# M3 before M4 in the lower half of layers two and three of a graph network, with two small products issued at later steps

## The chip, the cores and the metric

The kernel runs on one core of a Trainium2 chip. The metric is device time in microseconds (us) of one launch, which computes all 16 batches; the profile is one execution taken by the hardware profiler. Engines are called as in the profile: PE (TensorE; PEld its weight loads), DVE (VectorE), ACT (ScalarE), POOL (GpSimd) and SP (whose queue issues most DMAs). All data are 32-bit floats.

## The reference

Inputs are nodes x (16 x 1024 x 128), a sparse-patterned adjacency adj (16 x 1024 x 1024) and the weights of two networks, each followed by a residual sum and a layer norm:

```python
# first network
degree = adj.sum(-1)[:, :, None]
h = einsum('bid,bij->bjd', x, adj) / degree
x = layernorm(x + relu(concat([x, h]) @ W.T + b))
# second network, four layers of this form
src_agg = einsum('bjv,bij->biv', nodes @ ws + bs, l2norm(adj, 2))   # rows normalised
dst_agg = einsum('bjv,bji->biv', nodes @ wd + bd, l2norm(adj, 1))   # columns normalised
nodes = tanh(concat([src_agg, nodes @ wn + bn, dst_agg]) @ wu + bu)
# layers three and four also get earlier features concatenated
x = layernorm(x + nodes)
```

Each batch thus needs two scaled copies of its adjacency: one with columns divided by their norms (`a` in the kernel), one transposed with rows divided by theirs (`at`). The norms come from sums of squares of the rows (`cols`, on ACT) and of the columns (`acc`, on POOL).

## The kernel before, in words

Batches run one after the other, and while one batch is in its layers two and three, the next one's adjacency is loaded, squared, summed and scaled. Order is written by hand for PE, DVE, ACT and POOL: every engine executes its instructions in the order in which the Python code issues them. The stages of a batch on PE are: messages and products of layer one, of layer two, of layer three, then the first network of the next batch (`pa`, L417 to L431), then messages and products of layer four.

**Messages** (`messages`, L488). For four groups of two node blocks a matmul `pt` (L498) makes the messages, DVE adds a bias (L501), giving the tiles `t`. Then DVE makes sums of message blocks that the products need: S3 (L515), S1 (L516, in place in `t`), S2 (L517), S4 (L518), in this order. Each holds two parts, SRC and DST, of 64 columns for each of four blocks: one for the row-normalised and one for the column-normalised adjacency. The functions called through `between` are issued after the DVE addition of a group: in layer three `sums3`, which waits for POOL's last sum of squares, transposes it (L261) and reduces it to `part` (L266).

**Products** (`aggregate`, L553). The adjacency product is done in a form of Strassen's and Winograd's, with seven products of half-size blocks (M1 to M4, Z11, Z12, Z21) over combined quarters (T on the column side, Q on the row side). PE's array is used in two halves of 64 columns: a list `upper` and a list `lower` of matmuls are zipped, and each step issues one matmul of each (L669 to L677). In the trace every such matmul is two records, so a step has two pairs of records. With n the number of feature tensors (1 in layer two, 2 in layer three, 3 in layer four), a stage begins with 2n `own` steps (the node's own term), followed by 24 steps. The upper half runs M1 in 8 steps, M2 in 8, the SRC part of M3 in 4, Z21; the lower half runs M4 in 8 steps (into the PSUM tile Ck), the DST part of M3 in 4 (into Dk), then Z12 and Z11. Event functions read results at steps counted from the end of the own steps: at 8 `m1_read` (L584, L585) and `m4_read` (L588, L589) on ACT, at 12 a copy of Dk into half of `e1` on ACT (L655), at 16 `m2_read` (L592 on DVE, L593 on ACT) and the sum of the two halves on DVE (L649), at 20 `m3_read` (L596, L597) and `second_half` (L600 takes Z1 out of its PSUM bank, L601, then tanh on ACT, L690). The last half ends with L679.

**Hooks** of a stage are functions that are issued at a step counted with the own steps. Layer two of each batch but the last has the sums for the next adjacency (`sums`, L233): for each of eight row blocks the squares on ACT (L248, and a copy with a sum, L245, for the first four), degrees on DVE (L247) for the other four, and running sums on POOL (L250, L252). Layer three has:

- step 1, `inverses3` (L284): the product `pc` of the column sums on PE, three small DVE operations (L290, L292, L297), and a power on POOL (L298), which gives the inverse norms of rows and columns;
- step 5, `factors`: DMAs of node blocks; three small DVE operations (L316, L317, L319), a DMA of the inverses to DRAM (L321) and two DMAs that spread them as the row `cinv` (L327);
- step 10, `factors_of_rows` (L300): `spread` on DVE (L303), its product `rp` on PE (through L179), and the copy `rinv` on DVE (L309);
- step 11 a transpose on DVE (L338), and at 12, 15, 19 and 25 four scalings each of the next adjacency by `cinv` on DVE (L333).

`rinv` is used first in layer four, where ACT scales rows with it (L454). The first product of `pa` writes the PSUM bank of Z1 and so waits for L600.

Of the kernel before, what the change touches and what calls it, by code (L numbers as in the profile page):

```python
# [15 lines left out]
NL = 4  # L16
# [7 lines left out]
def adj_resnorm_kernel(ctx: ExitStack, tc: tile.TileContext, x, adj, w0, b0, layers, out):  # L24
# [33 lines left out]
    nc = tc.nc  # L58
# [10 lines left out]
    NJ = NB // 2  # L69
# [103 lines left out]
    def small(name, shape=(K,)):  # L173
        return ps_s.tile([P, *shape], F32, tag="small", name=name)
# [6 lines left out]
    def product(name, i=None):  # L181
        if i is None:
            return ps_t.tile([P, HW], F32, tag="pt", name=name)
        return ps_p.tile([P, HW], F32, tag=f"p{i}", name=name)
# [115 lines left out]
    def row_inverses(b, inv):  # L300

        spread = one.tile([P, NH, G, BPH], F32, tag="own", name=f"sp{b}")
        nc.vector.tensor_mul(spread, inv[:, :NB].rearrange("p (h k) -> p h k", h=NH)[:, :, None, :]  # L303
                             .to_broadcast([P, NH, G, BPH]),
                             group[:, None, :, None].to_broadcast([P, NH, G, BPH]))
        pr = small(f"rp{b}")
        by_halves(pr, fold, spread.rearrange("p h g k -> p (h g k)"))
        rinv = one.tile([P, K], F32, tag="rinv", name=f"rinv{b}")
        nc.vector.tensor_copy(rinv, pr)  # L309
        return rinv  # L310
# [169 lines left out]
    def combine(i, y, T):  # L480
# [4 lines left out]
        else:  # L485
            nc.vector.tensor_sub(T[4], y[1, 0], T[2])

    def messages(b, l, feats, wm, between={}, with_sums=True):  # L488


        nch = CHUNKS[l]
        t = [one.tile([P, NJ, 2, 2, V], F32, tag=f"t{j}", name=f"t{l + 1}_{b}_{j}") for j in range(2)]
        for n, g in enumerate((2, 3, 0, 1)):
            pt = ps_t.tile([P, 2, 2 * P], F32, tag="pt", name=f"pt{l + 1}_{b}_{g}")
            for q in range(2):
                i = 2 * g + q
                for k, (f, c) in enumerate(feats):
                    nc.tensor.matmul(pt[:, q], f[:, i * P:(i + 1) * P], wm[:, 1 + c],  # L498
                                     start=(k == 0), stop=(k == nch - 1))
            j, o = divmod(2 * g, NJ)  # L500
            nc.vector.tensor_add(t[j][:, o:o + 2].rearrange("p k a v c -> p k (a v c)"), pt,  # L501
                                 wm[:, 0][:, None, :].to_broadcast([P, 2, 2 * P]))
            if n in between:
                between[n]()
        if not with_sums:
            return t


        s = slice(1 if l == 0 else 0, 2)
        S = {i: one.tile([P, NJ, 2, V], F32, tag=f"S{i}", name=f"S{i}_{l + 1}_{b}") for i in (2, 3, 4)}  # L510
        X = {(v, j): t[j][:, :, :, v] for v in range(2) for j in range(2)}
        S[1] = X[1, 0]
        if l == 0:
            nc.vector.tensor_sub(S[2][:, 0:2, 0], X[0, 0][:, 0:2, 0], X[1, 0][:, 0:2, 0])
        nc.vector.tensor_sub(S[3][:, :, s], X[0, 0][:, :, s], X[1, 0][:, :, s])  # L515
        nc.vector.tensor_add(S[1][:, :, s], X[1, 0][:, :, s], X[1, 1][:, :, s])  # L516
        nc.vector.tensor_sub(S[2][:, :, s], S[1][:, :, s], X[0, 0][:, :, s])  # L517
        nc.vector.tensor_sub(S[4][:, :, s], X[0, 1][:, :, s], S[2][:, :, s])  # L518
        return X, S

    SRC, DST = 0, 1

    def plain_layer(b, l, feats, t, a, at, fT, etag, hooks):

# [28 lines left out]
    def aggregate(b, l, feats, msgs, a, at, T, Q, fT, etag, hooks={}, pieces=1):  # L553


        w = wown[l]
        n = len(feats)
        X, S = msgs
        Y = {DST: quarters(a), SRC: quarters_t(at)}
        TT = {DST: T, SRC: Q}  # L560
        low, high = slice(0, V), slice(V, P)
        Z0, Z1 = (product(f"z{h}_{l}_{b}", h) for h in range(NH))
        A, Bk, Ck = (product(f"m{i}_{l}_{b}") for i in range(3))
        e0 = one.tile([P, HW], F32, tag="e0", name=f"e0_{l}_{b}")
        e12 = one.tile([P, 2, HW], F32, tag=etag, name=f"e12_{l}_{b}")
        e1, e2 = e12[:, 0], e12[:, 1]
# [7 lines left out]
        def prod(name, part):  # L574
            y, t = Y[part], TT[part]
            x, y = {"M1": lambda: (X[0, 0], y[0, 0]), "M2": lambda: (S[2], t[2]), "M3": lambda: (S[3], t[3]),
                    "M4": lambda: (S[1], y[0, 1]), "Z11": lambda: (X[0, 1], y[1, 0]),
                    "Z12": lambda: (S[4], y[1, 1]), "Z21": lambda: (X[1, 1], t[4])}[name]()
            return [(x[:, k, part], y[:, k]) for k in range(NJ)]
# [7 lines left out]
        def m4_read():  # L587
            nc.scalar.copy(e2[high], Ck[low])  # L588
            nc.scalar.copy(e2[low], Ck[low])  # L589
# [15 lines left out]
        if l == 0:  # L605
            upper = [
                (Z1, True, own(1, 1)), (Z0, True, own(1, 0)),
                (Z1, False, [src(1, 1, j) for j in range(2, NB)]),
                (A, True, prod("M1", DST)), (Bk, True, prod("M2", DST)), (A, True, prod("M3", DST)),
                (Z0, False, prod("Z21", DST) + [src(1, 0, j) for j in range(NB)]),  # L610
            ]
            lower = [
                (Z1, True, own(0, 1)), (Z0, True, own(0, 0)),
                (Z1, False, [(S[2][:, j, SRC], at[1][:, j]) for j in range(2)] + [src(0, 1, j) for j in range(2, NB)]),
                (Ck, True, prod("M4", DST) + [src(1, 1, j) for j in range(2)]),
                (Z1, False, prod("Z12", DST)),
                (Z0, False, prod("Z11", DST) + [src(0, 0, j) for j in range(NB)]),
            ]
            def m4_and_m2_read():
                m4_read()  # L620
                m2_read()

            def m3_and_second_half():
                m3_read()
                second_half()

            events = {10: m1_read, 14: m4_and_m2_read, 18: m3_and_second_half}
        else:
            Dk = product(f"m3_{l}_{b}")
            upper = [  # L630
                (Z1, True, own(1, 1)), (Z0, True, own(1, 0)),
                (A, True, prod("M1", DST) + prod("M1", SRC)), (Bk, True, prod("M2", DST) + prod("M2", SRC)),
                (A, True, prod("M3", SRC)),
                (Z0, False, prod("Z21", SRC) + prod("Z21", DST)),
            ]
            lower = [
                (Z1, True, own(0, 1)), (Z0, True, own(0, 0)),
                (Ck, True, prod("M4", DST) + prod("M4", SRC)), (Dk, True, prod("M3", DST)),
                (Z1, False, prod("Z12", SRC) + prod("Z12", DST)),
                (Z0, False, prod("Z11", SRC) + prod("Z11", DST)),  # L640
            ]

            def first_reads():
                m1_read()
                m4_read()

            def m2_and_half_of_m3():
                m2_read()
                nc.vector.tensor_add(e0[high], e0[high], e1[high])  # L649

            def last_reads():
                m3_read()
                second_half()

            events = {8: first_reads, 12: lambda: nc.scalar.copy(e1[high], Dk[low]), 16: m2_and_half_of_m3,  # L655
                      20: last_reads}

        def steps(groups, rows):
            flat = []
# [85 lines left out]
    inv = two.tile([P, C], F32, tag="inv", name="inv0")  # L745
# [152 lines left out]
    for b in range(B):  # L898
        nxt = b + 1 < B
        n = b + 1  # L900
        y, yt = quarters(a), quarters_t(at)
        st = {}
# [5 lines left out]
        if b == 0:  # L908
            def first_half0():
                nonlocal rinv  # L910
                to_x1(0)
                rinv = row_inverses(0, inv)
                column_reduce(0, st0, acct)
                for q in (2, 3):
                    scale_rows(rows[q], q, rinv)
# [38 lines left out]
            def folded(l, part):  # L954
                return lambda *_: part(l, fetched[l])

            hooks = {1: lambda *_: inverses(0, st0, NB), 3: rows0, 4: folded(1, fold_begin), 6: folded(1, fold_end),
                     7: cinv0, 9: lambda *_: fold_and_scale(2, 0), 11: second0, 12: folded(2, fold_end),
                     14: lambda *_: fold_and_scale(3, 1), 18: first0, 20: folded(3, fold_end), 26: sums0}
# [5 lines left out]
        else:  # L965
# [3 lines left out]
            w = {"ys": summed(f"y{nm}")}  # L969
# [24 lines left out]
            def end1(w=w):  # L994
# [3 lines left out]
            hooks = {0: begin1, 7: scale1, 12: centre1, 17: squares1, 19: rstd1,  # L998
                     22: lambda: combine_1(yt), 25: end1, 28: lambda: combine(2, yt, Q)}
# [13 lines left out]
        hooks = {0: quarters2}  # L1013
# [9 lines left out]
        w = {}  # L1023
# [13 lines left out]
            w["cinv"] = factor_row(n, st, 1, "cinv")  # L1037

        def factors_of_rows(w=w):
            w["rinv"] = row_inverses(n, st["inv"])  # L1040

        def scale(i, h):
            scale_columns(a2, w["cinv"], range(i, i + NJ), half(h))

        hooks, between = {}, {}
        if nxt:
            between = {1: sums3}
            hooks = {1: inverses3, 5: factors, 10: factors_of_rows, 11: start3, 12: lambda: scale(0, 1), 15: lambda: scale(NJ, 1), 19: lambda: scale(0, 0),
                     25: lambda: scale(NJ, 0)}
        t = messages(b, 2, feats, wm, between)  # L1050
        wm = message_weights(b, 3)
        aggregate(b, 2, feats, t, a, at, T, Q, f23, "acc", hooks)
        if nxt:
            dinv = factor_row(n, st, 2, "dinv")
            yT = first_gnn(n, w["xn"], w["xT"], a2, dinv)
            rinv = w["rinv"]
# [96 lines left out]
    b = B - 1  # L1153
# [48 lines left out]
```

## Time and profile before

| quantity | value |
|---|---|
| three timed runs | 2528.31, 2528.6, 2529.8 us; median 2528.6 |
| profiled execution | 2525.06 us, span 2523.3 us, granted PE clock 0.999 |
| busy: PE, DVE, ACT, POOL | 2498.0, 1652.3, 836.5, 523.8 us |
| products of layer one, in batches 1 to 14 | 27.85 us |
| products of layer two, all batches | 26.54 to 26.55 us |
| products of layer three, batches 0 to 14 | 27.92 to 29.28 us, mean 28.65 |
| the same in batch 15, which has no hooks there | 27.62 us |
| products of layer four, batches 0 to 14 | 29.43 us |

The stages are measured from their first matmul to that of the following stage, in the timeline of PE. In a line of the timeline stand start, duration, engine, line of the kernel, operation, output and input, number of instructions, and in brackets how long the engine had been idle and what ended that. In a line of the waits stand the waiting engine, tile and line, then the releasing engine, tile and line, total us, number of times and the longest. The chain of work gives start, duration and what ran. Batches are counted from 0.

### The profile page before, as it was taken

The page shows a single profiled execution, that of the slowest core. Times are in us where ns is not written, and L with a number is a line of the kernel's source. Part 1 is how long each engine was busy: PE and PEld are TensorE (multiplying, and loading weights), DVE is VectorE, ACT ScalarE, POOL GpSimd, SP SyncE. Part 2 cuts the span into 40 slices and gives each one's busy share as a digit, 9 for nine tenths or more (in the row PEclk, how much of TensorE's full clock was granted, in tenths as well). Part 3 has the DMA queues.
Part 4 walks back from the last instruction along what each step waited for, and adds up shares of the span by engine and source line. Part 5 has one row for each costly group of instructions (what it writes and reads, how often), then busy time and mean ns, then how long its engine had stood idle before and what let it go on. Part 6 is the DMA issues. An engine that isn't in the chain of part 4 may idle for free.

```text
span 2523.3 us, 30190 instructions
## 1 busy us (share of the span) xinstructions
PE 2498.0 (99%) x11693; PEld 1158.6 (46%) x11693; DVE 1652.3 (65%) x1982; ACT 836.5 (33%) x1553; POOL 523.8 (21%) x217
## 2 busy tenths in 40 slices
PE   8999999999999999999999999999999999999998
PEld 4544445444454444544435454344544445444454
DVE  5858566585665757667576575765758567585643
ACT  5414333142331513324133251432414333142311
POOL 5401204012040221302113030130301204012000
PEclk9999999999999999999999999999999999999999
DMA  9417254271543615436163451725417255271410
GB/s 203 98 44 148 53 99 99 51 143 40 101 101 68 129 34 109 99 65 125 34 124 83 84 107 47 132 64 100 95 45 148 53 97 102 51 143 40 92 23 9
DMA packets 358736, 219.63 MB, mean 87 GB/s; under 512 B 148929, under 2 KB 329409, under 8 KB 358593
## 3 DMA queue, kind: packets, MB, share of 16 engines
q1 hardware_dynamic: 357184, 213.51, 41.8%
q0 software_dynamic: 1408, 4.20, 0.7%
q8 instruction: 92, 1.51, 0.3%
q14 instruction: 52, 0.42, 0.1%
HBM read 199.17 MB, written 18.46 MB: 86 GB/s over the span
## 4 chain that ended last, share of the span: by engine, by line
PE 67%; DVE 9%; SPq 5%; POOL 5%; DMA 4%; issue 4%; ACT 4%; DVEq 0%; POOLq 0%; ACTq 0%
PE m L677 26%; PE z L677 19%; PE pt L498 10%; PE pa L179 8%; SPq L231 5%; DMA a<-in_adj_dram 3%; POOL acc L252 2%; PE pw L179 2%; POOL inv L298 2%; ACT sq L248 1%; DVE e L601 1%; DMA out_dram<-y 1%; POOL acc L250 1%; ACT sq L245 1%; DVE cols L247 1%
## 5 line engine op out<-in xcount | busy, mean ns | idle before, releaser
L375 POOL TENSOR_TENSOR rs<-ve,mhalf 128x32 f32<-128x32 f32 x30 | 162.8, 5428 | 1388.5 <-DVE ve L373 1388.5
L677 PE MATMUL z<-at,t 128*64 128x512 f32 x1224 | 383.7, 592 | 0.0
L677 PE MATMUL m<-Q,S 128*64 128x512 f32 x768 | 337.4, 592 | 0.0
L501 DVE TENSOR_TENSOR t<-pt,wm 128x512 f32<-128x512 f32 x256 | 175.4, 690 | 177.7 <-PE pt L498 177.3
L677 PE MATMUL m<-T,S 128*64 128x512 f32 x1008 | 290.9, 593 | 0.0
L677 PE MATMUL m<-a,t 128*64 128x512 f32 x1008 | 266.6, 594 | 0.0
L252 POOL TENSOR_TENSOR acc<-acc,sq 128x1024 f32<-128x1024 f32 x90 | 221.3, 2459 | 130.6 <-ACT sq L248 127.0
L677 PE MATMUL z<-a,S 128*64 128x512 f32 x504 | 228.3, 593 | 0.0
L677 PE MATMUL z<-a,t 128*64 128x512 f32 x504 | 226.8, 592 | 0.0
L677 PE MATMUL z<-T,t 128*64 128x512 f32 x504 | 226.8, 592 | 0.0
L454 ACT ACTIVATE a<-a,rinv 128x256 f32<-128x256 f32 x480 | 198.2, 495 | 54.9 <-DMA a<-in_adj_dram 47.0
L677 PE MATMUL m<-at,t 128*64 128x512 f32 x828 | 214.5, 593 | 0.0
L333 DVE TENSOR_TENSOR a<-a,cinv 128x512 f32<-128x512 f32 x250 | 156.5, 696 | 88.1 <-DMA cinv<-dr 84.4
L498 PE MATMUL pt<-wm,f1T 128*128 128x256 f32 x768 | 213.6, 383 | 0.1
L179 PE MATMUL pa<-a,xn 128*64 128x512 f32 x960 | 208.6, 592 | 0.2 <-DVE e L600 0.2
L677 PE MATMUL z<-at,S 128*64 128x512 f32 x444 | 200.8, 592 | 0.0
L584 ACT COPY e<-m 64x512 f32<-64x512 f32 x63 | 36.6, 582 | 473.5 <-PE m L677 473.1
L677 PEld LDWEIGHTS z<-at,t 128*64 128x64 f32 x1224 | 120.8, 137 | 130.7 <-issue 111.3
L677 PEld LDWEIGHTS m<-Q,S 128*64 128x64 f32 x768 | 105.2, 137 | 164.3 <-issue 146.2
L677 PE MATMUL z<-Q,t 128*64 128x512 f32 x384 | 172.6, 592 | 0.0
L677 PEld LDWEIGHTS m<-T,S 128*64 128x64 f32 x1008 | 102.4, 137 | 144.4 <-issue 123.9
L498 PEld LDWEIGHTS pt<-wm,f1T 128*128 128x128 f32 x768 | 143.3, 190 | 44.3 <-issue 19.9
(197 smaller groups left out, 3698.3 us busy)
## 6 DMA issues: line engine op xcount, KB each, us to landing
a<-in_adj_dram SPq DMA_DIRECT2D x120, 512.0 KB, 12.7
a<-in_adj_dram SPq DMA_DIRECT2D x480, 128.0 KB, 4.1
xn<-in_x_dram SPq DMA_DIRECT2D x128, 64.0 KB, 2.0
wm<-wsave SPq DMA_DIRECT2D x16, 512.0 KB, 3.8
wm<-wsave SPq DMA_DIRECT2D x31, 256.0 KB, 3.3
xs<-in_x_dram SPq DMA_DIRECT2D x60, 128.0 KB, 3.5
cinv<-dr SPq DMA_DIRECT2D x30, 256.0 KB, 5.1
dinv<-dr SPq DMA_DIRECT2D x30, 256.0 KB, 5.1
```

The source lines that it names most:

```text
L179: nc.tensor.matmul(out[s], x[:, s], y, start=start, stop=stop)
L231: nc.sync.dma_start(ov[g, :, ks], ys[g * C:(g + 1) * C, ks])
L245: nc.scalar.activation(sq, a[:, i, :], AF.Copy, accum_out=degree)
L252: nc.gpsimd.tensor_add(acc, acc, sq)
L298: nc.gpsimd.tensor_tensor(inv[:, s], cols[:, s], mhalf[:, s], ALU.pow)
L333: engine.tensor_mul(a[:, i, s], a[:, i, s], cinv[:, s])
L375: nc.gpsimd.tensor_tensor(rstd, ve, mhalf[:, :n], ALU.pow)
L454: nc.scalar.activation(st[:, k], st[:, k], AF.Copy, scale=rinv[:, q * QB + k:q * QB + k + 1])
L498: nc.tensor.matmul(pt[:, q], f[:, i * P:(i + 1) * P], wm[:, 1 + c], start=(k == 0), stop=(k == nch - 1))
L501: nc.vector.tensor_add(t[j][:, o:o + 2].rearrange("p k a v c -> p k (a v c)"), pt, wm[:, 0][:, None, :].to_broadcast([P, 2, 2 * P]))
L584: nc.scalar.copy(e0[high], A[high])
L677: nc.tensor.matmul(o, x, y, start=start, stop=stop)
```

## The change

In layers two and three the lower half takes the DST part of M3 first (4 steps) and then M4 (8 steps); layer four keeps M4 first. The reads at the events are exchanged with them: at 8, after `m1_read`, the copy of Dk; at 12 `m4_read`. S3 is made in two DVE operations, the DST part before the SRC part, in layers two, three and four (in layer one there is only the DST part, as before). In layer three, `inverses3` is issued at step 4 instead of 1; `row_inverses` is cut in two, with `spread` at step 10 as before and the product `rp` with the copy `rinv` at step 18, between the second and the third group of scalings.

```diff
         nc.vector.tensor_mul(spread, ...)
+        return spread
+
+    def gather_inverses(b, spread):
         pr = small(f"rp{b}")
         by_halves(pr, fold, spread.rearrange("p h g k -> p (h g k)"))
         rinv = one.tile([P, K], F32, tag="rinv", name=f"rinv{b}")
...
-        nc.vector.tensor_sub(S[3][:, :, s], X[0, 0][:, :, s], X[1, 0][:, :, s])
+        for part in (DST, SRC) if l else (DST,):
+            nc.vector.tensor_sub(S[3][:, :, part], X[0, 0][:, :, part], X[1, 0][:, :, part])
...
+            first_of_lower = [(Ck, True, prod("M4", DST) + prod("M4", SRC)), (Dk, True, prod("M3", DST))]
+            reads_of_lower = [m4_read, m3_half]
+            if l < NL - 1:
+                first_of_lower.reverse()
+                reads_of_lower.reverse()
...
             lower = [
                 (Z1, True, own(0, 1)), (Z0, True, own(0, 0)),
-                (Ck, True, prod("M4", DST) + prod("M4", SRC)), (Dk, True, prod("M3", DST)),
+                *first_of_lower,
...
             def first_reads():
                 m1_read()
-                m4_read()
+                reads_of_lower[0]()
...
-            events = {8: first_reads, 12: lambda: nc.scalar.copy(e1[high], Dk[low]), 16: m2_and_half_of_m3,
-                      20: last_reads}
+            events = {8: first_reads, 12: reads_of_lower[1], 16: m2_and_half_of_m3, 20: last_reads}
...
         def factors_of_rows(w=w):
-            w["rinv"] = row_inverses(n, st["inv"])
+            w["spread"] = row_inverses(n, st["inv"])
+
+        def factors_gathered(w=w):
+            w["rinv"] = gather_inverses(n, w["spread"])
...
-            hooks = {1: inverses3, 5: factors, 10: factors_of_rows, 11: start3, 12: lambda: scale(0, 1), 15: lambda: scale(NJ, 1), 19: lambda: scale(0, 0),
-                     25: lambda: scale(NJ, 0)}
+            hooks = {4: inverses3, 5: factors, 10: factors_of_rows, 11: start3, 12: lambda: scale(0, 1),
+                     15: lambda: scale(NJ, 1), 18: factors_gathered, 19: lambda: scale(0, 0), 25: lambda: scale(NJ, 0)}
```

More of the change, by code (lines that the diff above doesn't have):

```diff
@@ L486, in combine @@
             nc.vector.tensor_sub(T[4], y[1, 0], T[2])
+    SRC, DST = 0, 1
     def messages(b, l, feats, wm, between={}, with_sums=True):
@@ L519, in messages @@
         return X, S
-    SRC, DST = 0, 1
     def plain_layer(b, l, feats, t, a, at, fT, etag, hooks):
@@ L629, in aggregate, with m3_half @@
             Dk = product(f"m3_{l}_{b}")
+            def m3_half():
+                nc.scalar.copy(e1[high], Dk[low])
+            first_of_lower = [(Ck, True, prod("M4", DST) + prod("M4", SRC)), (Dk, True, prod("M3", DST))]
[3 more added lines that the diff above has]
+                reads_of_lower.reverse()
             upper = [
@@ L911, in first_half0 @@
                 to_x1(0)
-                rinv = row_inverses(0, inv)
+                rinv = gather_inverses(0, row_inverses(0, inv))
                 column_reduce(0, st0, acct)
```

## The prediction, as it was put down before the result was known

> **What bounds the kernel now.** I read the page's engine shares first, then the waits, then the timeline of one batch (number 2, layers two and three, from 398.97 us), then the chain of work at the end of its layer three.
>
> ```profile
> PE 2498.0 (99%) x11693; PEld 1158.6 (46%) x11693; DVE 1652.3 (65%) x1982; ACT 836.5 (33%) x1553; POOL 523.8 (21%) x217
> ...
> PEld rp L179 <- DVE sp L303: 18.1, 15, 1.3
> PEld pc L179 <- DVE part L266: 13.7, 15, 1.4
> DVE a L333 <- DMA cinv<-dr: 84.4, 15, 6.7
> ```
>
> TensorE is busy 99% of the span, so only its gaps can be won. Two waits stand once in each batch that prepares a next one (15): rp, the product of the row inverses, and pc, that of the column sums.
>
> ```profile
> 433.96 0.31 PE L179 MATMUL pc<-part,fold 128*64 128x32 f32 x4 [0.26 <-DVE part L266]
> ...
> 442.44 0.31 PE L179 MATMUL rp<-sp,fold 128*64 128x32 f32 x4 [0.40 <-DVE sp L303]
> ```
>
> Matmuls overlap, so bracketed idle time understates what is lost. Records of one half of the array start 0.43 us apart; upper and lower half run side by side. The pair before pc started at 433.10, so the next was due at 433.53: 0.43 lost. Before rp, 441.43 + 0.43 = 441.86: 0.58 lost. A third loss has no wait row:
>
> ```profile
> 399.81 0.69 DVE L515 TENSOR_TENSOR S<-t 128x512 f32<-128x512 f32 x1
> 400.53 0.69 DVE L516 TENSOR_TENSOR t<-t,t 128x512 f32<-128x512 f32 x1
> ...
> 400.74 3.82 PE L677 MATMUL m<-a,t 128*64 128x512 f32 x15
> ...
> 404.39 0.59 PE L677 MATMUL m<-a,t 128*64 128x512 f32 x1
> ...
> 436.71 3.61 PE L677 MATMUL m<-a,t 128*64 128x512 f32 x16
> ```
>
> In layer three 16 records of M1 and M4 start within 3.61 - 0.59 = 3.02 us; in layer two they need 404.39 - 400.74 = 3.65. M1 starts on time, but M4's operand (L516) ends at 401.22, so the lower half trails by 0.63 us, to the end of the stage: the layer-two products take 26.54 us in every batch, 60 pairs of records x 0.429 = 25.74.
>
> The last view shows what waits behind those gaps:
>
> ```profile
> 450.84 7.31 DVE L333 TENSOR_TENSOR a<-a,cinv 128x512 f32<-128x512 f32 x12 [6.70 <-DMA cinv<-dr]
> ...
> 460.35 0.69 DVE e L596
> 461.04 0.03 issue
> 461.07 0.70 DVE e L600
> 461.77 0.04 issue
> 461.81 1.50 PE pa L179 x5
> ```
>
> The next stage, pa, starts 0.05 us after L600, which frees its PSUM bank. L600 stands behind a chain on other engines: squares on ACT, sums on POOL (to 431.4), transpose, column sums, power on POOL, two DMAs, twelve scalings, L592, L649, L596.
>
> **What the Trainium skill says.** *SBUF — State Buffer*, "Who interferes with whom": a VectorE instruction with two SBUF inputs and a GpSimd instruction that reads SBUF exclude each other, the later one blocking for the whole of the earlier. The trace agrees: L601 takes 2.42 instead of 0.69 us where it meets a running sum of POOL (L252, 2.36). *VectorE: DVE Perf Modes*, "The DRAIN you can't avoid": the next operation waits until the pipe is empty, unless it is not held. Here waited neighbours L515 and L516 start 0.725 us apart for 0.69 of work, unwaited scalings 0.60.
>
> **The change, part by part.** The batches' stages are measured between first matmuls in the timeline.
>
> 1. *M3 first in layer two* (16 batches). M3's first products need only the DST half of S3: it begins at 399.81, takes 0.42 (the 128x256 form) and is there at 400.23, 0.5 before 400.74. M4 comes four steps (3.4 us) later, long after its operand. Gain on PE: 0.63 each. In layer three M4 wasn't late (its operand ended at 436.55, before 436.71), so there the swap gives nothing.
>
> 2. *The split of S3* in layers two to four: two of 0.42 for one of 0.69. Half to half isn't waited, some 0.33 apart, half to L516 0.45 (both from layer one's rows): 0.78 for 0.725, +0.06 on DVE. In layer four it hides under six own steps (5.1 us). In layer three it lies in the chain to L600.
>
> 3. *pc to step 4.* Part is finished 1.3 us after the stage begins, step 4 comes at 3.4: the wait goes. Its readers on DVE follow the S sums anyway (437.92), so nothing behind them moves.
>
> 4. *rp to step 18.* The spread is ready 9.8 us after the stage begins; step 18 comes at 15.5: the wait goes. Its copy to rinv (L309) now stands on DVE between scalings 8 and 9, ahead of L592 and L600: 0.11 us (from its start to the next operation's, as before). SP and POOL keep their order. pc and rp together: the stage lasts 28.65 us in the mean of the 15, against 27.62 in the batch without hooks plus 0.28 for the eight short matmuls: 0.75 each.
>
> 5. *The reads on ACT in layer two.* One copy (L655) stands where two stood (L588, L589), so the square behind it ends 0.60 earlier, while L593, behind all of them, keeps its time:
>
> ```profile
> 416.93 1.06 ACT L248 ACTIVATE sq<-a 128x1024 f32<-128x1024 f32 x1
> ...
> 418.10 0.62 ACT L593 COPY e<-e 64x512 f32<-64x512 f32 x1
> ...
> 416.44 7.66 POOL L252 TENSOR_TENSOR acc<-acc,sq 128x1024 f32<-128x1024 f32 x3 [2.27 <-ACT sq L248]
> ...
> 418.75 0.69 DVE L649 TENSOR_TENSOR e<-e,e 64x512 f32<-64x512 f32 x1 [3.31 <-ACT e L593]
> ...
> 422.23 2.42 DVE L601 TENSOR_TENSOR e<-e 128x512 f32<-128x512 f32 x1
> ```
>
> POOL's first sum would run 415.86 to 418.22, the second from about 418.3 to 420.65. L649 is released at 418.75, now inside the second (before, it slipped between two); it would end some 0.55 after it, 421.2 instead of 419.44. Batch 0 shows this meeting already: L649 takes 2.68 there. Behind it L247, L596 and L600 move 1.76 back, but L601 then meets no sum: 421.2 + 2.69 + 0.10 + 0.69 = 424.7, against 424.65. So the sharing takes the delay in, and the chain leaves layer two +0.05. Bounds: -0.6 if the earlier square is passed on whole, +1.76 if L649's delay is.
>
> *Sum.* PE alone would win 16 x 0.63 + 15 x 0.75 = 21.3 us. But pa can't start before L600. L600 ends before pa by 0.05 (batches 2 and 6) to 1.26 us, 0.83 in the mean; less the 0.05, 0.78 of room. Its chain hangs on layer one, by the load of the next adjacency and its squares, not on PE in layers two and three, so PE's gain doesn't move it; it grows by 0.05 + 0.06 + 0.11, with rounding 0.25. The gain per batch is the room less this: 0.53, or 15 x 0.53 = 8.0, less 0.1 for batch 1, where PE's own path ends last; plus 0.63 in the last batch, which has no chain: **8.5 us**. Against the profiled span, 2523.3 - 8.5 = 2514.8; the timed runs are 5.3 longer (median 2528.6), so 2520.1.
>
> **Rivals.**
> - *The full gain.* The chain shortens because squares and sums start earlier: at -0.4 per batch instead of +0.25, 0.65 x 15 more, capped by PE's path in several: 16 us in all, 2512.6. For it: POOL waits 2.27 and 2.48 us for squares. Against: the last two squares stand behind L601's tanh, which doesn't come earlier.
> - *No change.* The chain eats the room, growing 0.8 instead of 0.25: 15 x (0.78 - 0.8) + 0.6, about 2528. For it: DMA landings scatter (L600's place varies by 2.4 us over the batches). Against: no added work of that size.
> - *Slower.* On DVE in layer two POOL's next sum goes ahead of the waiting L649 once more, 2.36 us per batch, all of it in the chain: 15 x (0.78 - 0.25 - 2.36) + 0.6 = -26.8, 2555. Decides from a growth of 0.82 us (1.16 for 0.2%). Against: in batch 0 L649 got in after one sum.
> - *M3 doesn't start on DST alone*: if it waits for both halves (the second ends at 399.81 + 0.33 + 0.42 = 400.56, and a weight load is 0.14), the lower half trails by less than 0.1. Since L600 bounds nearly all batches, that costs under 0.5 us: 2520.5.
>
> **How the numbers follow.** 0.2% is 5.1 us, about what measurement can tell from no change. The forecast, with M3's rival, gets 0.57, its own range 2515.5 to 2524.5 (growth from 0 to 0.5); the full gain 0.14; no change 0.20; slower 0.09. Faster: 0.55 of the first and the full gain, 0.69; same 0.22; slower 0.09. The range leaves out the slower rival and the ends of the others: 2511 to 2527.5.
>
> **What would show it.** Right: layer two's products 25.9 us in place of 26.54; no waits of pc and rp; pa 0.05 us after L600 in nearly all batches, with PE's gap now there, in layer three; L649 near 2.4 us and L601 at 0.69 in layer two; L309 between scalings. Wrong: layer two still 26.5; L600 more than 0.5 us later against the start of layer two, or earlier (the full gain); new gaps in layers four or one, where nothing waits now.

## The result, and the profile after

The changed kernel takes 2519.31 us (median of 6 runs, 2518.91 to 2522.89) against 2528.45 us (6 runs, 2525.58 to 2529.91) of the kernel before, run beside it: a ratio of 0.9967, 95% interval 0.9954 to 0.998. It is faster, by 9.1 us; 8.5 were forecast. The profiled span fell less, from 2523.3 to 2517.5 us, because the profiled execution of the kernel before (2525.06 us) was faster than all its timed runs. In the two later measurements the same change gained 7.2 and 6.0 us (ratio 0.9975 in both).

Lines have moved by some: L588, L589 (reads of M4) are now L592, L593, the copy of Dk L655 is L636, the half sum L649 is L663, L592 and L596 are L596 and L600, L600 is L604, L601 is L605, the tanh L690 is L703, the matmuls of the products L677 are L690, the scalings L333 are L336, the copy to rinv L309 is L312. In text about a changed kernel the new numbers are used. The description counts 24 steps behind the own ones; they are 28 (Z21 and Z11 have eight), which with the two own steps of layer two makes the 60 pairs of records that the prediction counts with.

The page's engine shares, kernel after:

```profile
PE 2487.2 (99%) x11693; PEld 1051.9 (42%) x11693; DVE 1661.8 (66%) x2030; ACT 836.3 (33%) x1553; POOL 519.8 (21%) x217
```

DVE has 48 instructions more, the second halves of S3 in 16 batches and three layers. PE's busy time fell by 10.8 us with the same number of matmuls; 16 x 0.64 = 10.2 us is what layer two's products lost. The share of 99% says as little as before. The waits, kernel after (waiting engine, tile, line, then the releaser; total us, times, longest):

```profile
DVE a L336 <- DMA cinv<-dr: 91.9, 15, 7.5
...
ACT f23T L703 <- DVE e L605: 27.9, 32, 0.9
ACT e L636 <- DMA out_dram<-y: 26.6, 13, 3.0
...
PEld pa L179 <- DVE e L604: 23.4, 15, 2.8
...
PE pa L179 <- DVE e L604: 10.2, 14, 2.0
...
PEld pt L503 <- ACT f23T L703: 5.6, 11, 1.3
```

The rows in which pc waits for part and rp for sp are gone. In their place stands pa, 15 times, waiting for L604, the operation that frees Z1's bank (L600 before). PE's timeline in layer two of batch 2, which starts at 398.04:

```profile
399.80 0.59 PE L690 MATMUL m<-a,t 128*64 128x512 f32 x1
399.81 0.59 PE L690 MATMUL m<-T,S 128*64 128x512 f32 x1
400.23 0.59 PE L690 MATMUL m<-a,t 128*64 128x512 f32 x1
400.24 0.59 PE L690 MATMUL m<-T,S 128*64 128x512 f32 x1
```

Upper and lower half (M1 reads `a` and `t`, M3 `T` and `S`) now start 0.01 us apart, and stay so. DVE makes the two halves of S3 from 398.87 to 399.63. The products of layer two take 25.90 us in all 16 batches, against 26.54. The chain of work that ends with the start of pa, batch 2, kernel after (start, duration, what ran):

```profile
458.65 0.70 DVE e L663
459.35 0.03 issue
459.38 0.02 DVEq L600
459.40 0.04 issue
459.45 0.69 DVE e L600
460.14 0.03 issue
460.17 0.70 DVE e L604
460.87 0.04 issue
460.91 1.50 PE pa L179 x5
```

L604 ends at 460.87 and pa starts at once. Before, that held in 2 of the 15 batches that prepare a next one (0.83 us in the mean); now it holds in all 15 (0.06). So TensorE has become fast enough, and the chain on the other engines sets the time. The stages, mean of batches 0 to 14, us:

| stage | before | after |
|---|---|---|
| products of layer two | 26.54 | 25.90 |
| messages of layer three | 7.10 | 7.38 |
| products of layer three, with the wait ahead of pa | 28.65 | 28.62 |
| pa | 17.27 | 17.32 |
| products of layer four | 29.43 | 29.43 |

Layer one and four don't change. Layer two gives 0.64, but 0.28 of it come back in the messages of layer three (to 8.23 instead of 7.10 in batch 12): PE comes earlier to its wait for the tanh L703 (the row of pt above, L503 is the matmul of the messages), which still comes when L605 releases it. Layer three takes as long as before: what pc and rp no longer cost is waited for ahead of pa. The four stages add up to 79.56 us before and 79.22 after; unrounded they differ by 0.355. With the last batch (0.64) that is 15 x 0.355 + 0.64 = 6.0 us. The profiled execution after reached its first layer two 0.2 us later (90.11 instead of 89.93), which leaves the 5.8 us by which the spans differ.

The link in layer two that the prediction worked out (item 5) reads like this, in views of batch 2. ACT before, with the two copies of M4 ahead of the next square:

```profile
412.90 0.58 ACT L588 COPY e<-m 64x512 f32<-64x512 f32 x1
413.49 0.58 ACT L589 COPY e<-m 64x512 f32<-64x512 f32 x1
413.97 1.05 ACT L245 ACTIVATE sq<-a 128x1024 f32<-128x1024 f32 x1
```

ACT after:

```profile
411.51 0.58 ACT L636 COPY e<-m 64x512 f32<-64x512 f32 x1 [1.69 <-DMA out_dram<-y]
412.10 1.06 ACT L245 ACTIVATE sq<-a 128x1024 f32<-128x1024 f32 x1
...
413.28 1.06 ACT L248 ACTIVATE sq<-a 128x1024 f32<-128x1024 f32 x1
...
416.69 0.62 ACT L597 COPY e<-e 64x512 f32<-64x512 f32 x1
```

POOL and DVE after:

```profile
414.57 7.57 POOL L252 TENSOR_TENSOR acc<-acc,sq 128x1024 f32<-128x1024 f32 x3 [3.47 <-ACT sq L248]
```

```profile
417.34 2.58 DVE L663 TENSOR_TENSOR e<-e,e 64x512 f32<-64x512 f32 x1 [2.84 <-ACT e L597]
...
421.93 0.69 DVE L604 TENSOR_TENSOR e<-e,z 128x512 f32<-128x512 f32 x1
422.72 0.69 DVE L605 TENSOR_TENSOR e<-e 128x512 f32<-128x512 f32 x1
```

L663 is released inside POOL's second sum and takes 2.58 us in place of 0.69; L605, which took 2.42 before, takes 0.69. The work on the next row block starts 0.59 us behind the first copy instead of 1.07, so 0.48 earlier (in all 15 batches), not 0.60. From the first copy of the lower half on ACT to the end of L605, batches 1 to 14 take 11.90 us in the mean, against 11.74.

### The profile page after: what moved, and what is told of

The parts are those of the page before. It is cut to its first block, busy times and chain, and to the rows that moved or that the text cites. A ratio compares the mean times of both kernels' runs of the same rounds, so it can differ in the third digit from the quotient of the medians.

```text
span 2517.5 us, 30270 instructions
## 1 busy us (share of the span) xinstructions
PE 2487.2 (99%) x11693; PEld 1051.9 (42%) x11693; DVE 1661.8 (66%) x2030; ACT 836.3 (33%) x1553; POOL 519.8 (21%) x217
## 4 chain that ended last, share of the span: by engine, by line
PE 59%; DVE 12%; DMA 9%; SPq 7%; ACT 4%; POOL 4%; issue 2%; DVEq 0%; POOLq 0%; ACTq 0%
PE m L690 22%; PE z L690 16%; PE pt L503 10%; PE pa L179 8%; SPq L231 7%; DMA a<-in_adj_dram 4%; DVE a L336 3%; DMA cinv<-dr 2%; POOL acc L252 2%; PE pw L179 2%; DMA out_dram<-y 2%; DVE e L663 2%; POOL inv L298 1%; ACT sq L248 1%; DMA dr<-invt 1%
## 5 line engine op out<-in xcount | busy, mean ns | idle before, releaser
L690 PE MATMUL m<-T,S 128*64 128x512 f32 x1008 | 395.8, 593 | 0.0
L690 PE MATMUL z<-at,t 128*64 128x512 f32 x1224 | 383.7, 592 | 0.0
L690 PE MATMUL m<-a,t 128*64 128x512 f32 x1008 | 366.7, 594 | 0.0
L690 PE MATMUL m<-Q,S 128*64 128x512 f32 x768 | 339.2, 593 | 0.0
L690 PE MATMUL m<-at,t 128*64 128x512 f32 x828 | 311.2, 592 | 0.0
L690 PE MATMUL z<-a,S 128*64 128x512 f32 x504 | 228.3, 593 | 0.0
L690 PE MATMUL z<-a,t 128*64 128x512 f32 x504 | 226.8, 592 | 0.0
L690 PE MATMUL z<-T,t 128*64 128x512 f32 x504 | 226.8, 592 | 0.0
L336 DVE TENSOR_TENSOR a<-a,cinv 128x512 f32<-128x512 f32 x250 | 157.6, 696 | 95.8 <-DMA cinv<-dr 91.9
L179 PE MATMUL pa<-a,xn 128*64 128x512 f32 x960 | 209.3, 594 | 10.2 <-DVE e L604 10.2
L503 PE MATMUL pt<-wm,f1T 128*128 128x256 f32 x768 | 213.7, 383 | 0.1
L690 PE MATMUL z<-at,S 128*64 128x512 f32 x444 | 202.6, 593 | 0.0
L690 PEld LDWEIGHTS m<-Q,S 128*64 128x64 f32 x768 | 104.1, 137 | 206.8 <-issue 206.3
L588 ACT COPY e<-m 64x512 f32<-64x512 f32 x63 | 36.6, 581 | 449.1 <-PE m L690 448.7
L690 PEld LDWEIGHTS m<-T,S 128*64 128x64 f32 x1008 | 117.8, 137 | 159.8 <-issue 158.1
L690 PE MATMUL z<-Q,t 128*64 128x512 f32 x384 | 172.6, 592 | 0.0
L690 PEld LDWEIGHTS z<-at,t 128*64 128x64 f32 x1224 | 120.7, 137 | 121.1 <-issue 111.4
L690 PEld LDWEIGHTS m<-a,t 128*64 128x64 f32 x1008 | 110.0, 137 | 125.9 <-issue 120.1
```

The costliest lines, as they stand in the source:

```text
L179: nc.tensor.matmul(out[s], x[:, s], y, start=start, stop=stop)
L336: engine.tensor_mul(a[:, i, s], a[:, i, s], cinv[:, s])
L588: nc.scalar.copy(e0[high], A[high])
L690: nc.tensor.matmul(o, x, y, start=start, stop=stop)
```

## The experiments

To compare kernels along the chain, the mean of the 15 batches is taken, in us from the start of the products of layer two. "Copy" is ACT's first copy of the lower half, "scalings" the first of them, "free" the end of the operation that frees Z1's bank, "room" the time from there to pa, and the last column counts the batches in which it is under 0.1. Products are those of the layer; msg. 3 are the messages of layer three.

| kernel | copy | scalings | free | room | under 0.1 | products 2 | msg. 3 | products 3 |
|---|---|---|---|---|---|---|---|---|
| before | 13.53 | 50.54 | 61.46 | 0.83 | 2 | 26.54 | 7.10 | 28.65 |
| after | 13.70 | 50.83 | 61.84 | 0.06 | 15 | 25.90 | 7.38 | 28.62 |
| after, second | 13.96 | 51.21 | 62.23 | 0.05 | 15 | 25.90 | 7.60 | 28.79 |
| after, third | 13.86 | 51.08 | 62.10 | 0.05 | 15 | 25.90 | 7.52 | 28.74 |
| M3 only | 13.85 | 51.00 | 61.93 | 0.91 | 1 | 25.90 | 7.51 | 29.42 |
| later steps only | 13.75 | 50.55 | 61.57 | 0.12 | 11 | 26.55 | 7.13 | 28.02 |
| later steps only, second | 13.81 | 50.62 | 61.64 | 0.09 | 13 | 26.55 | 7.11 | 28.08 |
| rinv last | 13.81 | 51.01 | 61.93 | 0.05 | 15 | 25.90 | 7.47 | 28.61 |
| a square later | 13.90 | 51.37 | 62.40 | 0.05 | 15 | 25.90 | 7.75 | 28.80 |
| bank freed first | 13.78 | 50.93 | 59.55 | 1.57 | 1 | 25.90 | 7.46 | 27.76 |
| before, bank freed first | 13.67 | 50.91 | 59.42 | 2.99 | 0 | 26.55 | 7.12 | 28.75 |
| and a degree later | 13.89 | 50.45 | 59.06 | 1.72 | 1 | 25.90 | 7.12 | 27.76 |
| and M4 first again | 13.77 | 49.45 | 58.07 | 3.34 | 0 | 26.55 | 7.10 | 27.75 |
| outputs not stored | 12.39 | 49.69 | 60.70 | 0.69 | 5 | 25.90 | 7.21 | 28.28 |

Each row comes from one profiled execution. That of the kernel before (2525.06 us) lies 3.4 to 5.7 us below the medians of its timed runs, so timed gains are in part larger than the table's. Ratios are to the kernel before, run beside each group on the same chip, with 95% intervals. Diffs are against the changed kernel.

**M3 only.** The products go back to steps 1 and 10; M3 stays first.

```diff
-            hooks = {4: inverses3, 5: factors, 10: factors_of_rows, 11: start3, 12: lambda: scale(0, 1),
-                     15: lambda: scale(NJ, 1), 18: factors_gathered, 19: lambda: scale(0, 0), 25: lambda: scale(NJ, 0)}
+            hooks = {1: inverses3, 5: factors, 10: lambda: (factors_of_rows(), factors_gathered()), 11: start3, 12: lambda: scale(0, 1),
+                     15: lambda: scale(NJ, 1), 19: lambda: scale(0, 0), 25: lambda: scale(NJ, 0)}
```

> The change without its two moved hooks: M3 first and S3 in two parts, but pc at step 1 and rp at step 10 as before. Theory (PE's gain in layer two is caught again by work that hangs on the other engines' chain): layer two's products fall to 25.9 us, but pc and rp wait for the chain and not for PE, so the 0.6 us come back as longer waits of pc and rp and nothing is won except 0.6 us in the last batch; with the chain some 0.2 us later per batch the time is 0 to 4 us above before. Rival (gains add up part by part): 16 x 0.64 = 10 us below before.

2531.51 us, +1.0: ratio 1.0007 (0.9998 to 1.0015). That the parts simply add up (the rival) is refuted. Layer two still gives its 0.64, but the waits, against 13.7 and 18.1 us before, show where it goes:

```profile
PEld pc L179 <- DVE part L266: 24.1, 15, 1.9
...
PEld rp L179 <- DVE sp L303: 20.4, 15, 1.4
```

Part and sp come from the chain, which doesn't start earlier. TensorE comes to pc sooner and waits there; the messages and products of layer three together take 36.93 us in place of 35.75. That is 0.54 us more than layer two gives, 8 us over the kernel, where the timed medians differ by 1.0: the profiled execution of this kernel was the slowest of its 13 (2533.38 us).

**Later steps only.** M4 first again and S3 in one operation; the products stay at steps 4 and 18.

```diff
-        for part in (DST, SRC) if l else (DST,):
-            nc.vector.tensor_sub(S[3][:, :, part], X[0, 0][:, :, part], X[1, 0][:, :, part])
+        nc.vector.tensor_sub(S[3][:, :, s], X[0, 0][:, :, s], X[1, 0][:, :, s])
...
-            if l < NL - 1:
+            if l < 0:
```

> The two moved hooks without the rest: M4 first and S3 in one piece as before, pc at step 4, rp at step 18. Theory: the waits of pc and rp go, PE is then bound by L600 in about half the batches and by itself (61.55 us from the start of layer two's products to pa) in the others; L600 comes 0.1 us later (rinv's copy): 5 to 8 us below before. Rival (gains add up): 11 us below before, and together with the other part the whole of 21.

2519.39 us, -11.1: ratio 0.9959 (0.9947 to 0.9972). More than the expected 5 to 8: half of the change gives as much as the whole. Layer two, messages, products of layer three and pa add up to 26.55 + 7.13 + 28.02 + 17.52 = 79.22 us; after, it is 25.90 + 7.38 + 28.62 + 17.32 = 79.22. They come to the same sum in different ways, and in part by chance. With the later steps alone the bank is free 0.27 us earlier (61.57 for 61.84), but pa takes 0.20 longer. PE's own work is on the path here too: in four batches the lower half of layer three still has a product to start when pa begins, as in batch 6:

```profile
1078.04 0.59 PE L689 MATMUL z<-a,t 128*64 128x512 f32 x1
1078.19 0.64 PE L179 MATMUL pa<-a,xn 128*64 128x512 f32 x1
1078.46 0.59 PE L689 MATMUL z<-a,t 128*64 128x512 f32 x1
```

Which of the two products, pc or rp, carries the gain was not tried apart. The kernel was run again in the third group, beside the whole change:

> The two moved hooks alone, once more and beside the changed kernel. Theory (M3 first buys nothing while the chain bounds pa, and its earlier square costs the chain 0.15 us): 0 to 4 us below the changed kernel, apart from what the landing of the store differs between the runs. Rival (M3 first is worth its 0.64 us per batch here too): 10 us above the changed kernel.

> The changed kernel beside the following ones: 7 to 11 us below before, pa 0.05 us after L600 in all 15 batches.

2519.49 us (0.9963, 0.995 to 0.9975) against 2523.0 us (0.9975, 0.9965 to 0.9985): the later steps alone are 3.5 us below the whole, whose -6.0 fell just short of the 7 to 11 expected. So no gain of M3 first is seen here; the medians are 3.5 us apart, with overlapping intervals.

**Bank freed first.** The third group of four scalings goes from step 19 to 25, behind the operation that frees the bank; the fourth stood there already.

```diff
-                     15: lambda: scale(NJ, 1), 18: factors_gathered, 19: lambda: scale(0, 0), 25: lambda: scale(NJ, 0)}
+                     15: lambda: scale(NJ, 1), 18: factors_gathered, 25: lambda: (scale(0, 0), scale(NJ, 0))}
```

> The changed kernel with the third group of scalings issued at step 25, behind the last reads, instead of at step 19 before them: the read that frees the PSUM bank for pa (L600 before) comes four scalings, 2.4 us, earlier on DVE. Theory (pa is bound by that read in the changed kernel): the gap ahead of pa goes, from layer two to pa 61.0 to 61.4 us instead of 61.9 in the mean, 7 to 13 us below the changed kernel, some 16 to 22 below before. Rival (the gap ahead of pa has another cause, the scaled adjacency or the node blocks): no change against the changed kernel, or pa's second half now waits for its scalings and all is lost again.

2507.29 us, ratio 0.9911 (0.9898 to 0.9925). The same edit in the kernel before:

> The kernel before with only that move of the third group of scalings. Theory: before the change PE was bound by pc and rp and by L600 in only two batches of 15 (0.3 and 0.1 us), so the same move is worth under 1 us here: within 0.1% of before. Rival (L600 bounded the kernel before as well): 5 us or more below before.

2527.78 us, 0.9988 (0.9982 to 0.9995): -2.7 us, a little more than expected, against -23.2 us with the change in place. In the changed kernel the bank is free 2.3 us earlier and pa starts 1.57 us behind it in the mean. In the timelines of batch 3 of the changed kernel with the bank freed first, DVE and PE:

```profile
609.29 0.69 DVE L604 TENSOR_TENSOR e<-e,z 128x512 f32<-128x512 f32 x1
610.09 0.69 DVE L605 TENSOR_TENSOR e<-e 128x512 f32<-128x512 f32 x1
610.70 3.69 DVE L336 TENSOR_TENSOR a<-a,cinv 128x512 f32<-128x512 f32 x6
```

```profile
611.05 0.59 PE L690 MATMUL z<-a,t 128*64 128x512 f32 x1
611.48 0.59 PE L690 MATMUL z<-T,t 128*64 128x512 f32 x1
611.48 0.59 PE L690 MATMUL z<-a,t 128*64 128x512 f32 x1
611.91 1.46 PE L179 MATMUL pa<-a,xn 128*64 128x512 f32 x6
```

L604 ends at 609.98 with the scalings behind it. PE goes through its last products without a gap, a pair each 0.43 us, and pa follows the last by 0.43 as well, 1.93 us after the bank came free. So L604 bound the changed kernel, and L600 hardly bound the one before.

**The same again, and rinv last.** The changed kernel, and with it one in which the product rp and its copy stand at step 26, behind all scalings (`18: factors_gathered` becomes `26: factors_gathered`).

> The changed kernel once more, beside the following ones. Theory: pa starts 0.05 us after L600 in all 15 batches again; 8 to 11 us below before.

> The changed kernel with rp and the copy rinv issued at step 26, behind all scalings and behind L600, instead of at step 18 between scalings. Theory (the copy stands in the chain that bounds pa): from the first scaling to the end of L600 10.9 us instead of 11.0, and 1.5 us below the changed kernel in all. Rival (its place doesn't matter): from the first scaling to L600 11.0 still.

2523.53 us (0.9975, 0.9965 to 0.9984) and 2521.89 us (0.9967, 0.9955 to 0.998). From the first scaling to the free bank it takes 10.93 us instead of 11.02, as before the change: the copy of rinv costs 0.1 us in each of 15 batches, 1.5 us, as worked out; the 1.6 us of the medians agree, within their intervals. The profiled spans differ by more (5.0 us), so it is the trace that shows the 0.1, not the medians.

The first of the two gained 2 us less than in the first measurement, and its profiled span is 7.3 us longer. The scalings start 0.38 later in each batch (51.21 for 50.83), 5.7 us in all, of which 0.26 lie already at the copy on ACT (13.96 for 13.70). Another 1.7 us lie in pa of batch 2, which takes 19.01 us instead of 17.32. PE's granted clock (PEclk) is halved there for 3.4 us, as the view of that stretch shows (busy time and instructions of PE, PEld, DVE, ACT and POOL, then PEclk, DMA share and GB/s):

```profile
462.80:466.20 3.40, 3.40 (x10) 0.97 (x8) 2.58 (x5) 1.06 (x2) 0.00 (x0) 0.50 0.03 9
466.20:470.00 3.80, 3.80 (x20) 1.29 (x18) 0.00 (x0) 0.00 (x0) 0.00 (x0) 1.00 0.41 114
```

**A square later.** The fourth row's sums go from step 13 to 14, behind the third copy, to take L663 out of POOL's way.

```diff
-                hooks[5 + 2 * i if i < 3 else 4 + 3 * i] = lambda i=i: sums(n, a2, st, (i,))
+                hooks[5 + 2 * i if i < 3 else 14 if i == 3 else 4 + 3 * i] = lambda i=i: sums(n, a2, st, (i,))
```

> The changed kernel with the squares of row block 3 in layer two issued at step 14, behind m4_read, instead of at 13 before it, so that they end 0.6 us later, as before the change. Theory (the earlier square makes POOL's second sum meet L649, and the sharing takes nearly all of that in): L649 takes 0.7 us again and L601 2.3, but L601 ends only 0.1 to 0.2 us earlier against the first copy of the lower half: 1 to 3 us below the changed kernel. Rival (L649's delay was passed on): L601 ends 1.5 us or more earlier, some 20 us below the changed kernel.

2528.13 us, 0.999 (0.9982 to 0.9998): 4.6 us slower than the changed kernel beside it, where 1 to 3 faster was expected. DVE in layer two of batch 2:

```profile
418.00 1.34 DVE L663 TENSOR_TENSOR e<-e,e 64x512 f32<-64x512 f32 x1 [2.91 <-ACT e L597]
...
422.13 2.42 DVE L605 TENSOR_TENSOR e<-e 128x512 f32<-128x512 f32 x1
```

The expectation overlooked that now three copies stand ahead of the square, not two as before the change. ACT's work on the row starts 1.55 us behind the first copy, later than before the change (1.07), L663 still meets a sum for a while, and L605 meets one too: 12.15 us from the copy to the end of L605, against 11.90. None of the three orders on ACT (11.74, 11.90, 12.15) is as much as 1.76 us from another.

**And a degree later.** The kernel with the bank freed first, and one of four row sums on DVE, which stood between L663 and L600 in layer two, goes into layer three's step 5.

```diff
-            else:
+            elif i != BPH + 1:
...
+            i = BPH + 1
+            nc.vector.reduce_sum(st["cols"][:, 2 * NB + i:2 * NB + i + 1], a2[:, i, :], axis=AX.X)
...
-                     15: lambda: scale(NJ, 1), 18: factors_gathered, 19: lambda: scale(0, 0), 25: lambda: scale(NJ, 0)}
+                     15: lambda: scale(NJ, 1), 18: factors_gathered, 25: lambda: (scale(0, 0), scale(NJ, 0))}
```

> The kernel with the third group of scalings behind the last reads, and in addition the degree of row block 5 summed on DVE in layer three, where DVE waits for POOL's power, instead of in layer two between L649 and the last reads. Theory (what is left of the gain is PE's wait in the messages of layer three for the tanh behind L601): L601 ends some 0.7 us earlier, the messages of layer three take 7.1 us again instead of 7.5, and the time is 4 to 6 us below that kernel's 0.991 of before, about 0.989. Rival (that wait hangs on something else): messages of layer three stay at 7.4 to 7.5.

2502.06 us, 0.9889 (0.9876 to 0.9903), the fastest of all. L605 ends 0.6 us earlier than with the bank freed first alone (25.21 instead of 25.81 us into layer two), the tanh comes earlier, and the messages of layer three take 7.12 us, as they did before the change.

**And M4 first again.** The same, without M3 first and without the split of S3 (both edits are shown above).

> The kernel with the scalings behind the last reads and the degree of row block 5 in layer three, but with M4 first and S3 in one piece as before the change. Theory (once the chain doesn't bind, M3 first is worth what PE gains by it): layer two's products 26.5 us instead of 25.9, 9 to 11 us above the same kernel with M3 first (0.989 of before), so about 0.993. Rival (M3 first is worth nothing): 0.989.

2511.01 us, 0.9929 (0.9916 to 0.9943). The two kernels were not run beside each other, but each beside the kernel before. The difference of the ratios, 0.004, is about 10 us; 16 x 0.65 = 10.4 us is layer two's part. So M3 first is worth its whole gain on TensorE where the chain doesn't bind, and while it does no gain of it was seen.

**Outputs not stored.** The outputs of batches 0 to 14 are not written.

```diff
-                store(b - 1, w["ys"], KS)
```

> The changed kernel without the store of the outputs of batches 0 to 14 (their y is made, but not written). Theory (in layer two ACT's first copy of the lower half waits for that store to land, since it writes the same buffer, and the whole chain to L600 hangs on it): the copy starts at 11.8 us of layer two instead of 13.7 to 14.0 in the batches with an early load, L600 ends more than 1 us earlier and no longer bounds pa: 12 to 20 us below the changed kernel. Rival (the chain hangs on the load of the adjacency and its squares alone): under 4 us below the changed kernel.

2511.47 us, 0.9929 (0.9915 to 0.9942), 11.5 us below the changed kernel beside it, just short of the 12 to 20 expected. ACT's copies in layer two of batch 1, which starts at 244.43:

```profile
255.02 0.58 ACT L588 COPY e<-m 64x512 f32<-64x512 f32 x1
255.63 0.58 ACT L589 COPY e<-m 64x512 f32<-64x512 f32 x1
256.23 0.58 ACT L636 COPY e<-m 64x512 f32<-64x512 f32 x1
```

L636 follows at once, 11.80 us after the stage begins; in the changed kernel (above) ACT stood idle for 1.69 us ahead of it, until the store had read the buffer that it writes (`e` of layer two and the stored `y` share one). The chain is thus fed by the landing of the store too: against the changed kernel beside it the copy comes 1.47 us earlier in the mean and the scalings 1.39. In 11 batches the copy comes at 11.8. In four (2, 6, 10 and 14) it comes at 14.0, because the squares ahead of it on ACT are late. These four and batch 0 are still bound by L604.

## Why the prediction was right

- *What bounds the kernel, and the sum's form*: right. The gain is the room ahead of L600, not the 21.3 us of TensorE. Freeing the bank first shows it from the other side: then the changed kernel, with the same work on PE, stands 23.2 us below the kernel before.
- *M3 first*: right in size (0.64 for 0.63), in all batches. Whether M3 needs both halves of S3 stays open: both are there at 399.63, 0.17 us before M3 starts, so the rival on it can't show itself.
- *The split of S3*, +0.06: the stages of the chain agree; it was not taken apart alone.
- *pc and rp*: right, both waits are gone; the copy of rinv costs 0.10 for 0.11. Their share on PE was put too low: without waits the stage lasts 27.76 us (bank freed first), so they cost 28.65 - 27.76 = 0.89, not 0.75. The last batch was no exact measure: there another product follows, 0.52 us after the last of layer three, where pa follows after 0.42, and the eight short matmuls take 0.23, not 0.28. It didn't matter, since the room set the gain.
- *The reads on ACT*: the picture was right (L649 inside one sum of POOL, L601 then free), the size not: +0.15 instead of +0.05, and L663 takes 2.58 instead of 2.4. The step that was mis-sized is "the square behind it ends 0.60 earlier": it comes 0.48 earlier, because the square started 0.48, not 0.60, behind the start of the second copy. POOL's sums, and L663 behind the second, come 0.1 later than worked out for that. The bounds of -0.6 and +1.76 are both refuted.
- *The chain's growth* is the term that was mis-sized: 0.38 (61.46 to 61.84) in place of 0.25. It is made of +0.17 at ACT's copy, +0.15 in layer two, +0.06 and +0.10 as forecast, and about -0.1 between L605 and the scalings, which was not taken apart. The first of these is not shown to come from the change: the copy waits for the landing of the store (in 10 of 15 batches before, 13 after), which the prediction left out ("Its chain hangs on layer one, by the load of the next adjacency and its squares"). Its mean lies between 13.70 and 13.96 in three profiles of the same changed kernel, and at 13.67 in the kernel before with the bank freed first, where it was 13.53 in the kernel before. In profiled spans that made the gain 5.8 instead of 8.5.
- *Not foreseen*: 0.28 us of the wait lies in the messages of layer three rather than ahead of pa, and pa itself takes 0.05 more. The first costs nothing, as long as L604 sets the start of pa.
- *The timed gain* of 9.1 us so close to 8.5 is partly luck: the prediction added 5.3 us to the span. Of these, 1.8 lie between span and time of one and the same execution, after the change as well; the other 3.5 stand for a profiled execution that was faster than the timed runs, while after the change the two agree (2519.26 and 2519.31). The span itself was forecast at 2514.8 and came out at 2517.5. The three measurements together put the gain at 6 to 9 us.
- *The rivals*: full gain, no change and slower all fall. The slower one needed POOL to pass L649 twice; in no batch does it take more than 2.68 us.

What the prediction didn't see is whose gain it is: with L600 as the bound the sum reads 0.63 + 0.75 per batch, capped, and either part alone might fill the cap. The runs show that the later steps do. By this sum M3 first alone should have won its 0.63 of 0.78 as well; it moves its gain into waits for the chain.

## What to carry to other kernels

When one engine's gaps are won, look for the operation that releases its next stage, and price the gain by the room ahead of it, not by the gap. Two parts that gain on the same engine are not alike: one that takes away a wait for the chain gives time, one that only brings the engine sooner to such a wait gives none until the chain is shortened. After such a change move the releasing operation ahead of work that nobody waits for yet (here four scalings, 14 to 16 us), and try the rest again.

## What the runs showed of the hardware that was not expected

A DVE operation that is released inside a POOL operation was let in ahead of POOL's next one, though POOL's records follow one another 0.08 us apart. The Trainium skill (*SBUF — State Buffer*, "Who interferes with whom") has the two exclude each other for the whole of an instruction, and the trace agrees; who comes next the runs show: in batch 2 POOL's second of three sums ends at 419.37, L663, released at 417.34, ends at 419.92, and POOL's third sum, recorded from 419.45, takes 2.69 us instead of 2.36. Over the 15 batches L663 takes 2.57 to 2.68 us, never the time of two sums.

PE's granted clock can halve behind such a wait, as in batch 2 above. It did so in four of the profiles, each time for 3.4 us within pa, which then took 19.01 us: in the second and third of the changed kernel and with a square later (batch 2), and with the outputs not stored (batch 6). In each it came about 1 us behind the longest wait for L604 of that execution: pa's first matmul started 2.58, 2.75, 2.97 and 3.10 us after the last product. Behind waits of 2.54 (the changed kernel's first profile) and 2.64 us (rinv last) it did not come. So a wait for the bank can cost 1.7 us on top of its own length; what sets it off was not tried.

The first pairs of pa after a wait are slower: the second pair of records starts 0.48 us after the first instead of 0.43, which makes the stage 0.05 us longer (17.32 for 17.27). It shows where PE stood idle for L604; the cause was not tried.
